# One column tiling for the matrix products of a triangle-attention stage

## The chip, the cores and the metric

The kernel runs on one core of one Trainium2 chip. The metric is the device time of one launch in microseconds (us), the median of several runs. Everything is computed in float32.

Of the engines, four matter here. TensorE (PE in the profile) multiplies matrices: a "stationary" operand is loaded into its array of 128 rows and 128 columns, and a "moving" operand streams through; results go to PSUM, an accumulation memory. VectorE (DVE) and GpSimd (POOL) do elementwise work, and ScalarE (ACT) does activations and copies.

## What is computed

Four images of 64 x 64 positions with 256 channels pass two layers. Layer 0 is a self-attention over the 4096 positions of an image (and isn't touched by the change). Layer 1 is a triangle attention followed by a small perceptron. Cut to what matters:

```python
# layer 0: x = x + attention(x) @ Wo + bo      (per image, 4096 tokens)
# layer 1, x_in = the result of layer 0, H = 8 heads of d_k = 32:
q, k, v1, v2 = (x_in @ W).reshape(B, N, N, H, d_k)   # for each of Wq, Wk, Wv1, Wv2
scores = einsum('bilhd,bljhd->biljh', q, k) / sqrt(d_k)
att = softmax(scores, axis=2)
out = einsum('biljh,bilhd,bljhd->bijhd', att, v1, v2)
h = x_in + out.reshape(B, N, N, E) @ Wo              # "hp" in the kernel
h = layer_norm(h)
mlp = relu(h @ W1 + b1) @ W2 + b2                    # "mp", then "zp"
return layer_norm(mlp + h)
```

The three-fold sum `out` is made by elementwise products of `att` and `v2` (tiles `R` on VectorE, `Rp` on GpSimd) that TensorE then sums with `v1` as its stationary operand (tile `acc`).

## The kernel before

The kernel orders its instructions by hand. While the triangle steps of image b run, the token part (hp, mp, zp: 16 tiles of 256 tokens for an image) of image b-1 runs beside them. This order repeats every two triangle steps, which the text calls a period; each period takes one tile of 256 tokens through the token part:

```python
ORDER = """
    r0/1 AO0/2 AO1/2 m1/1 RO4/2 RE5/1 SO/1 ... sp/1 ... z0/1 WO/1 ... z1/1 tO/1 ... tE ... h1/-1 ... h0/-1 ht
    ... m0 VE
""".split()      # R: product, A: accumulate, t: transposes of the weights, sp: scores,
                 # h0/h1: heads, ht: transposes of h, m0/m1: hidden, z0/z1: outputs
```

The triangle steps' work on TensorE. `accumulate` uses stationary operands of 128 rows and 32 columns, and four of them, each with its own 32 columns of the array and its own 32 partitions of PSUM, stand beside each other:

```python
def accumulate(self, step, m):
    ...
    for c in range(4):
        nc.tensor.matmul(
            acc[32 * c : 32 * c + 32, n % 2, :], w[:, n, c, 16 * h : 16 * h + 32],
            R[:, ts(c, 8), :].rearrange("p d j -> p (d j)"),
            start=n not in begun, stop=n in begun,
        )                                             # 512 moving columns

def turn_weights(self, step):                         # "att": full transposes
    for n in range(4):
        nc.tensor.transpose(att[:, n, :], e[...], ident)

def scores(self, pair, u):                            # "sp": 32 rows, 64 columns
    for n in range(8):
        for h in range(2):
            for lh in range(2):
                nc.tensor.matmul(sp[ts(h, 64), lh, n, :], k[rows, u * 8 + n, :], q[rows, u * 8 + n, :],
                                 start=True, stop=True)
```

The token part, with stationary operands of 128 columns and with transposes that add a residual to what a product has left in PSUM:

```python
def heads(self, tt, n, psum=pb, new=None):            # "hp", n = 0 and 1
    for cc in range(2):
        nc.tensor.matmul(hp[:, n, :], A[:, cc, ts(n, 2), :].rearrange("p i j -> p (i j)"), wo1_sb[:, cc, :],
                         start=(cc == 0), stop=False)
    for cc in range(2):
        nc.tensor.matmul(hp[:, n, ts(cc, P)], yc[:, cc, ts(n, P)], ident, start=False, stop=(cc == 1),
                         is_transpose=True)

def turn(self, tt):                                   # "htp"
    for cc in range(2):
        for n in range(2):
            nc.tensor.transpose(htp[:, cc, ts(n, P)], h[:, n, ts(cc, P)], ident)

def hidden(self, tt, fc, wide=False):                 # "mp", fc = 0 to 3
    for cc in range(2):
        nc.tensor.matmul(self.mp[:, fc % 2, :], w1_sb[:, cc, ts(fc, P)], self.hT[tt][:, cc, :],
                         start=(cc == 0), stop=(cc == 1))

def outputs(self, tt, n, apart=None, new=None):       # "zp", n = 0 and 1
    for fc in range(4):
        nc.tensor.matmul(zp[:, n, :], self.hid[tt][:, fc, ts(n, P)], w2_sb[:, fc, :],
                         start=(fc == 0), stop=(fc == 3 and tt not in self.hT2))
    if tt in self.hT2:
        for cc in range(2):
            nc.tensor.matmul(zp[:, n, ts(cc, P)], self.hT2[tt][:, cc, ts(n, P)], ident,
                             start=False, stop=(cc == 1), is_transpose=True)
```

Image 0 has no earlier image; beside its triangle steps (`first_layer1`) the kernel prepares layer 0 of the later images (`Ahead`): transposes of x ("tp"), values ("vp") and factors ("gf"):

```python
def values(self, s):                                  # "vp<-wh,xT"
    for n in range(4):
        for cc in range(2):
            nc.tensor.matmul(self.vp[:, ts(n, P)], self.xT[cc][:, ts(n, P)], wh_sb[:, cc, :],
                             start=(cc == 0), stop=(cc == 1))

def factors(ps, xT, t):                               # "gf", 32 stationary columns
    for w, wt in enumerate((wg_sb, wf_sb)):
        for cc in range(2):
            for n in range(4):
                nc.tensor.matmul(ps[32 * n : 32 * n + 32, w, :], wt[:, cc, :], xT[cc][:, ts(n, P)],
                                 start=(cc == 0), stop=(cc == 1))
```

The images follow one another; after the last one, `rest.alone` runs the token part of that image by itself:

```python
for b in range(NB):                                   # NB = 4
    L = layer0(b, F, safe, rest)
    ...
    if b == 0:
        first_layer1(L, ahead, F)
    else:
        next_layer1(b, L, rest, ahead, F)
    ...
rest.alone(NP * (NB - 1), NP * NB)
```

Of the kernel before, what the change touches and what calls it, by code (L numbers as in the profile page):

```python
# [16 lines left out]
P = 128  # L17
# [32 lines left out]
def attention_then_triangle_kernel(  # L50
# [6 lines left out]
    nc = tc.nc  # L57
# [13 lines left out]
    def pa(name):  # L71
        return psA.tile([P, 2, 512], F32, tag="a", name=name)

    def pb(name):
        return psB.tile([P, 512], F32, tag="b", name=name)
# [5 lines left out]
        return const.tile(shape, F32, tag=name, name=name)  # L81

    scale1 = 1.0 / math.sqrt(D)

# [212 lines left out]
    class Ahead:  # L299
# [32 lines left out]
        def values(self, s):  # L332
            self.vp = pb("vp")
            for n in range(4):
                for cc in range(2):
                    nc.tensor.matmul(
                        self.vp[:, ts(n, P)], self.xT[cc][:, ts(n, P)], wh_sb[:, cc, :],
                        start=(cc == 0), stop=(cc == 1),
                    )
# [38 lines left out]
    def layer0(b, F, safe, rest):  # L378
# [208 lines left out]
        for g in range(8 * NQB):  # L587
            qb, k = divmod(g, 8)
            if b == 0 and not safe:
                for load in later[3 * g : 3 * g + 3]:  # L590
                    load()
                if g == 6:
                    fold_bias()
                if g == 20:
                    add_b2()
            if safe and k == 0 and qb + 1 < NQB:
                mx, todo = pieces(qb + 1)
                for qc, t in todo:
                    max_piece(qc, t, mx)
                row[qb + 1] = max_row(mx)  # L600
            if g + 1 < 8 * NQB:
                scores(g + 1)
            values(g)

            if qb > 0 and not (qb == last and k >= 6):
                for part in parts[k]:
                    part(qb - 1)
            if qb == last and k == 3:
                L.fetch_v1(0)
                L.fetch_v1(1)  # L610
            if qb == last and k == 5:
                if b > 0:
                    rest.load(NP * (b - 1))
                L.fetch_qk(0, True)
# [47 lines left out]
        values1(1)  # L662
        score(2)
        hidden(0)
        score(3)
        proj(last, "q", 1, None, stage[1][:, 3, :], nc.scalar)
        L.sums(0)
        proj(last, "k", 1, None, stage[2][:, 0, :], nc.scalar)
        L.fetch_qk(1)
        L.weights(0)  # L670
        hidden(1)
        L.turn(0)
        L.stationary(0)
# [196 lines left out]
    class Tokens:  # L870
# [25 lines left out]
        def heads(self, tt, n, psum=pb, new=None):  # L896
            if n == 0 if new is None else new:
                self.hps[tt] = psum("hp").rearrange("p (n c) -> p n c", n=2)
            hp = self.hps[tt]
            A, yc = self.A[tt]  # L900
            for cc in range(2):
                nc.tensor.matmul(  # L902
                    hp[:, n, :], A[:, cc, ts(n, 2), :].rearrange("p i j -> p (i j)"), wo1_sb[:, cc, :],
                    start=(cc == 0), stop=False,
                )
            for cc in range(2):
                nc.tensor.matmul(
                    hp[:, n, ts(cc, P)], yc[:, cc, ts(n, P)], ident, start=False, stop=(cc == 1),
                    is_transpose=True,
                )  # L910


# [107 lines left out]
        def hidden(self, tt, fc, wide=False):  # L1020
            if wide and fc == 0:
                self.wide = pa("mp").rearrange("p o (f t) -> p o f t", f=2)
            if fc % 2 == 0:
                self.mp = self.wide[:, fc // 2] if wide else pb("mp").rearrange("p (f t) -> p f t", f=2)
            for cc in range(2):
                nc.tensor.matmul(  # L1026
                    self.mp[:, fc % 2, :], w1_sb[:, cc, ts(fc, P)], self.hT[tt][:, cc, :],
                    start=(cc == 0), stop=(cc == 1),
                )
            return self.mp  # L1030
# [8 lines left out]
        def outputs(self, tt, n, apart=None, new=None):  # L1039
            if n == 0 if new is None else new:  # L1040
                self.zp[tt] = pb("zp").rearrange("p (n c) -> p n c", n=2)
            zp = self.zp[tt]
            if apart is not None:
                zp = self.zp[tt + 1] = apart("zp").rearrange("p (n c) -> p n c", n=2)
            for fc in range(4):
                nc.tensor.matmul(  # L1046
                    zp[:, n, :], self.hid[tt][:, fc, ts(n, P)], w2_sb[:, fc, :],
                    start=(fc == 0), stop=(fc == 3 and tt not in self.hT2),
                )
            if tt in self.hT2:  # L1050
                for cc in range(2):
                    nc.tensor.matmul(
                        zp[:, n, ts(cc, P)], self.hT2[tt][:, cc, ts(n, P)], ident,
                        start=False, stop=(cc == 1), is_transpose=True,
                    )

        def finish(self, tt, eng=nc.gpsimd):
# [324 lines left out]
    def run(safe):  # L1382
        rest, ahead = Tokens(), Ahead()
        with tc.manual_schedule():
            F = front0(0)
            for b in range(NB):
                L = layer0(b, F, safe, rest)
                F = Front() if b + 1 < NB else None
                if F is None:

                    rest.ios.append(L.io)
                if b == 0:
                    first_layer1(L, ahead, F)
                else:
                    next_layer1(b, L, rest, ahead, F)
                if F is not None:
                    rest.ios.append(L.io)
            rest.alone(NP * (NB - 1), NP * NB)

    run(safe=False)  # L1400


# [11 lines left out]
    with tc.If(flag > 0):  # L1414
        run(safe=True)
# [33 lines left out]
```

## Time and profile before

| | before |
|---|---|
| time, median of 3 runs | 3816.12 us (3815.49 to 3818.42) |
| span of the profiled execution | 3813.2 us |
| PE busy | 3683.6 us (97%) |
| DVE busy | 2641.8 us (69%) |
| ACT busy | 1935.7 us (51%) |
| POOL busy | 1804.3 us (47%) |

The page of the profile gives each engine's busy time over the whole span, which mixes stages with different limits. Two more views split it: the busy time of each engine in a stretch of the span, and the chain of work that ended last, which follows the end of the program back to what released each step. A row such as `L1026 PE MATMUL mp<-hT,w 128*128 128x256 f32 x1024` reads: line 1026 of the kernel, TensorE, tile mp made from hT and w, stationary operand of 128 rows and 128 columns, moving operand of 128 partitions and 256 columns, 1024 records. The program has 512 such products before: the profile holds two records for a float32 product (two passes), and one for a float32 transpose. In the timeline, consecutive records of one kind are merged into a row, with the start first and the length second; as matmuls are pipelined, rows overlap, and the distance from one row's start to the next one's start is the time that the work took.

### The profile page before, as it was taken

Reading aid. Unit: us, or ns where it says so; the run is one execution under the profiler, and the core shown is the slowest. Engines: PE = TensorE matmul, PEld = TensorE weight load, DVE = VectorE, ACT = ScalarE, POOL = GpSimd, SP = SyncE. Lnnn points to the kernel's source line nnn. Section 1 sums busy time; section 2 is a strip of 40 time slices with the busy share of each in tenths; the row PEclk is TensorE's granted clock in tenths of the full one; section 3 lists DMA queues with packets and bytes.
Section 4 is the critical chain, followed back from the end, with each engine's and each line's share of the span. In section 5 each row is a group of like instructions: output and inputs, shape, how many; then the busy total and the mean of one; then the engine's idle time right before and its main releaser. Section 6 shows DMA issues by size and latency. Waiting matters only on the chain.

```text
span 3813.2 us, 60145 instructions
## 1 busy us (share of the span) xinstructions
PE 3683.6 (97%) x23498; PEld 1796.9 (47%) x23498; DVE 2641.8 (69%) x2050; ACT 1935.7 (51%) x4257; POOL 1804.3 (47%) x930
## 2 busy tenths in 40 slices
PE   9999988898999999999999999999999999999997
PEld 5444443443444455554344445555344445555476
DVE  4444488897544459999544548999754455999976
ACT  3333355554333357676333346766533335677654
POOL 4000088896000049999200008999600004999954
PEclk9999999999999999999999999999999999999999
DMA  4111355544111164323111143342211116431221
GB/s 117 54 50 49 97 140 139 150 114 152 36 47 53 50 151 92 86 57 94 62 47 50 50 125 89 81 95 70 92 42 47 50 60 142 95 89 48 69 61 51
DMA packets 439749, 309.43 MB, mean 81 GB/s; under 512 B 299360, under 2 KB 404576, under 8 KB 432160
## 3 DMA queue, kind: packets, MB, share of 16 engines
q1 hardware_dynamic: 419952, 291.12, 29.0%
q10 hardware_dynamic: 16240, 8.59, 0.9%
q0 software_dynamic: 3264, 5.78, 0.6%
q8 instruction: 188, 3.08, 0.4%
q14 instruction: 105, 0.86, 0.1%
HBM read 165.88 MB, written 139.46 MB: 80 GB/s over the span
## 4 chain that ended last, share of the span: by engine, by line
PE 81%; POOL 7%; issue 3%; DMA 3%; DVE 3%; ACT 3%; SPq 0%; ACTq 0%; POOLq 0%; DVEq 0%
PE o L453 24%; PE acc L843 17%; PE proj L510 8%; PE s L431 7%; POOL Rp L833 6%; PE mp L1026 5%; PE zp L1046 5%; PE sp L731 3%; PE v1p L535 3%; PE hp L902 2%; PE y L495 2%; DVE R L833 1%; PE att L785 1%; ACT S L741 1%; PE den L470 1%
## 5 line engine op out<-in xcount | busy, mean ns | idle before, releaser
L833 POOL TENSOR_TENSOR Rp<-attP,v 128x2048 f32<-128x2048 f32 x328 | 1490.1, 4574 | 462.4 <-DMA qk<-k 327.2
L833 DVE TENSOR_TENSOR R<-att,v 128x2048 f32<-128x2048 f32 x696 | 1548.9, 2274 | 113.7 <-PE acc L843 76.6
L460 DVE TENSOR_TENSOR esum<-esum,e 128x2048 f32<-128x2048 f32 x224 | 512.8, 2289 | 583.0 <-ACT e L442 579.8
L843 PE MATMUL acc<-R,wsel 128*32 128x512 f32 x5568 | 711.0, 605 | 44.2 <-DVE R L833 32.1
L442 ACT ACTIVATE e<-s 128x1024 f32<-128x1024 f32 x512 | 496.8, 1022 | 403.0 <-PE s L431 385.4
L954 POOL TENSOR_SCALAR nt<-mv 128x4 f32<-128x4 f32 (+1 forms) x51 | 9.9, 193 | 1283.3 <-DVE mv L919 1279.5
L453 PE MATMUL o<-e,vlo 128*128 128x512 f32 x1024 | 473.7, 605 | 0.0
L453 PE MATMUL o<-e,vhi 128*128 128x512 f32 x1024 | 472.6, 605 | 0.0
L853 ACT COPY ao<-acc 128x1024 f32<-128x1024 f32 x256 | 255.4, 1021 | 229.1 <-PE acc L843 202.5
L843 PE MATMUL acc<-Rp,wsel 128*32 128x512 f32 x2624 | 345.5, 600 | 21.3 <-POOL Rp L833 21.0
L843 PEld LDWEIGHTS acc<-R,wsel 128*32 128x32 f32 x5568 | 153.7, 110 | 381.5 <-issue 263.1
L453 PEld LDWEIGHTS o<-e,vlo 128*128 128x128 f32 x1024 | 184.0, 189 | 280.8 <-issue 280.8
L453 PEld LDWEIGHTS o<-e,vhi 128*128 128x128 f32 x1024 | 184.3, 189 | 279.7 <-issue 279.7
L431 PE MATMUL s<-gT,fT 32*128 32x512 f32 x2048 | 302.3, 640 | 4.3 <-ACT e L442 4.0
L768 ACT ACTIVATE es<-S,rd 128x64 f32<-128x64 f32 x1024 | 257.7, 336 | 10.2 <-DVE rd L760 7.0
L472 DVE RECIPROCAL rec<-den 128x512 f32<-128x512 f32 x32 | 107.4, 3357 | 215.6 <-PE den L470 215.6
L1046 PE MATMUL zp<-w,hid 128*128 128x256 f32 x1024 | 247.5, 387 | 7.2 <-ACT hid L1035 7.2
L1026 PE MATMUL mp<-hT,w 128*128 128x256 f32 x1024 | 249.5, 389 | 0.7 <-ACT hT L998 0.7
L1026 PEld LDWEIGHTS mp<-hT,w 128*128 128x128 f32 x1024 | 186.5, 190 | 101.4 <-ACT hid L1035 36.9
L1046 PEld LDWEIGHTS zp<-w,hid 128*128 128x128 f32 x1024 | 186.4, 191 | 71.9 <-issue 31.9
L522 ACT COPY st<-proj 128x512 f32<-128x512 f32 x104 | 61.0, 586 | 293.1 <-issue 165.9
L843 PEld LDWEIGHTS acc<-Rp,wsel 128*32 128x32 f32 x2624 | 81.1, 111 | 211.7 <-issue 140.6
(166 smaller groups left out, 3826.7 us busy)
## 6 DMA issues: line engine op xcount, KB each, us to landing
v<-v2d SPq DMA_DIRECT2D x24, 1024.0 KB, 12.5
v1c<-v1d SPq DMA_DIRECT2D x128, 128.0 KB, 2.8
aT<-ao SPq DMA_DIRECT2D x1024, 16.0 KB, 1.9
A<-aT SPq DMA_DIRECT2D x256, 64.0 KB, 2.1
out_dram<-z SPq DMA_DIRECT2D x63, 256.0 KB, 2.5
y<-yT SPq DMA_DIRECT2D x56, 256.0 KB, 2.1
q<-st SPq DMA_DIRECT2D x56, 256.0 KB, 2.5
v1d<-st SPq DMA_DIRECT2D x56, 256.0 KB, 2.2
```

What stands on the lines that cost most here:

```text
L431: nc.tensor.matmul(s_ps[r // 2][:, r % 2, :], fT[rows, tt, ts(n, P)], gT[rows, ts(qb, QB)], start=True, stop=not safe,)
L442: nc.scalar.activation(e[g][:, 2 * j : 2 * j + 2, :], s_ps[j], AF.Exp)
L453: nc.tensor.matmul(o_ps[qb], F.v[tt][:, r * 4 + n, :], es[:, r, :], start=(k == 0 and r == 0), stop=(k == 7 and r == 3),)
L460: nc.vector.tensor_tensor(esum[qb], esum[qb], es, ALU.add)
L510: nc.tensor.matmul(ps, w[:, cc, rows], y(qb, cc), start=(cc == 0), stop=(cc == 1))
L535: nc.tensor.matmul(ps[:, ts(n, C)], y(qb, cc)[:, ts(m * 2 + n, P)], wv1_sb[:, cc, :], start=(cc == 0), stop=(cc == 1),)
L768: nc.scalar.mul(e[:, i, :], rows[:, i, :], rec[:, i : i + 1])
L833: eng.tensor_tensor(R, src.unsqueeze(1).to_broadcast([P, D, N]), v2[:, h], ALU.mult)
L843: nc.tensor.matmul(acc[32 * c : 32 * c + 32, n % 2, :], w[:, n, c, 16 * h : 16 * h + 32], R[:, ts(c, 8), :].rearrange("p d j -> p (d j)"), ...
L853: nc.scalar.copy(self.ao[step][:, ts(np, 2)].rearrange("p k d j -> p k (d j)"), self.acc[step][np])
L1026: nc.tensor.matmul(self.mp[:, fc % 2, :], w1_sb[:, cc, ts(fc, P)], self.hT[tt][:, cc, :], start=(cc == 0), stop=(cc == 1),)
L1046: nc.tensor.matmul(zp[:, n, :], self.hid[tt][:, fc, ts(n, P)], w2_sb[:, fc, :], start=(fc == 0), stop=(fc == 3 and tt not in self.hT2),)
```

## The change

The products of the token part and of `values` are divided, wherever they run inside the triangle steps, into four products of 32 stationary columns each, so that TensorE's array has there the same division into four times 32 columns as for `accumulate`. The residuals, which were transposes, become ordinary products with the identity (divided in the same way). It is for having fewer changes of the array's division between neighbouring pieces of work. Outside the triangle steps (`tiling[0] = 1`) everything is as it was. The diff, with cuts marked:

```diff
+    tiling = [1]
+
+    def mm(out, lhsT, rhs, start, stop, residual=False):
+        m = P // tiling[0]
+        how = dict(is_transpose=True) if residual and tiling[0] == 1 else {}
+        for c in range(tiling[0]):
+            nc.tensor.matmul(out[ts(c, m)], lhsT[:, ts(c, m)], rhs, start=start, stop=stop, **how)
 ...                                            # Ahead.values
-                    nc.tensor.matmul(
+                    mm(
                         self.vp[:, ts(n, P)], self.xT[cc][:, ts(n, P)], wh_sb[:, cc, :],
 ...                                            # heads
-                nc.tensor.matmul(
+                mm(
                     hp[:, n, :], A[:, cc, ts(n, 2), :].rearrange("p i j -> p (i j)"), wo1_sb[:, cc, :],
                     start=(cc == 0), stop=False,
                 )
             for cc in range(2):
-                nc.tensor.matmul(
+                mm(
                     hp[:, n, ts(cc, P)], yc[:, cc, ts(n, P)], ident, start=False, stop=(cc == 1),
-                    is_transpose=True,
+                    residual=True,
                 )
 ...                                            # hidden
-                nc.tensor.matmul(
+                mm(
                     self.mp[:, fc % 2, :], w1_sb[:, cc, ts(fc, P)], self.hT[tt][:, cc, :],
 ...                                            # outputs: the products, and the residuals
-                nc.tensor.matmul(
+                mm(
                     zp[:, n, :], self.hid[tt][:, fc, ts(n, P)], w2_sb[:, fc, :],
 ...
-                    nc.tensor.matmul(
+                    mm(
                         zp[:, n, ts(cc, P)], self.hT2[tt][:, cc, ts(n, P)], ident,
-                        start=False, stop=(cc == 1), is_transpose=True,
+                        start=False, stop=(cc == 1), residual=True,
                     )
 ...                                            # the loop over images
+                tiling[0] = 4
                 if b == 0:
                     first_layer1(L, ahead, F)
                 else:
                     next_layer1(b, L, rest, ahead, F)
+                tiling[0] = 1
```

## The prediction

> **What bounds the kernel now.** I read the page first, then the chain of work that ended last, then the busy times by stretch, then the timeline of TensorE.
>
> ```profile
> PE 3683.6 (97%) x23498; PEld 1796.9 (47%) x23498; DVE 2641.8 (69%) x2050; ACT 1935.7 (51%) x4257; POOL 1804.3 (47%) x930
> ```
>
> TensorE is busy for 97% of the span, but the change touches only the triangle steps, so the question is what bounds those. The chain of waits shows it: in image 1 pieces of `acc` begin at 1429.59, 1457.35, 1485.11 ... 1707.21, that is every 27.76 us, and between them the chain stays on PE. From about 1729 us on it passes to POOL (59% of the chain from 1730 to 1785). Images 2 and 3 repeat this (PE from 2300 to 2629 and from 3201 to 3533). In image 0 (about 480 to 900) it hops between DMA, POOL, DVE, ACT and PE. The busy times of three stretches, one period of the first kind, one of the second, and two triangle steps of image 0; the columns after the length are PE, PEld, DVE, ACT, POOL:
>
> ```profile
> 1540.63:1568.39 27.76, 27.76 (x257) 14.96 (x260) 26.86 (x20) 19.65 (x55) 26.64 (x15) 1.00 0.20 49
> 1756.00:1783.20 27.20, 26.30 (x189) 13.09 (x189) 26.99 (x20) 17.60 (x53) 26.55 (x15) 1.00 0.32 88
> 600.00:626.20 26.20, 18.88 (x224) 8.56 (x224) 25.43 (x17) 13.60 (x36) 26.05 (x6) 0.99 0.85 189
> ```
>
> In the first PE is busy in all of 27.76 us, DVE is 0.90 us short of it, POOL 1.12. In the second PE has 0.9 us to spare (there are no more scores to make), and DVE and POOL are full. In image 0 PE idles for 7 of 26 us. So a change of PE's work counts in full in the first kind, about 12 periods in each of images 1 to 3 (1729 less 1400, over 27.76, is 11.9), 36 in all; in the others little of it.
>
> Now the first kind of period itself. Row by row the timeline of PE gives the work and, from one start to the next, its cost:
>
> ```profile
> 1545.85 0.66 PE L785 MATMUL att<-ident,es 128*128 128x128 f32 x4
> 1546.34 1.03 PE L902 MATMUL hp<-wo,A 128*128 128x256 f32 x4
> 1547.21 0.38 PE L907 MATMUL hp<-ident,yc 128*128 128x128 f32 x2
> 1547.43 1.03 PE L902 MATMUL hp<-wo,A 128*128 128x256 f32 x4
> 1548.29 0.38 PE L907 MATMUL hp<-ident,yc 128*128 128x128 f32 x2
> 1548.51 0.60 PE L993 MATMUL htp<-ident,h 128*128 128x128 f32 x4
> 1549.04 1.92 PE L843 MATMUL acc<-R,wsel 128*32 128x512 f32 x16
> 1550.78 1.04 PE L843 MATMUL acc<-Rp,wsel 128*32 128x512 f32 x8
> 1551.76 1.99 PE L1026 MATMUL mp<-hT,w 128*128 128x256 f32 x8
> 1553.68 1.92 PE L843 MATMUL acc<-R,wsel 128*32 128x512 f32 x16
> 1555.53 1.99 PE L1026 MATMUL mp<-hT,w 128*128 128x256 f32 x8
> 1557.46 1.98 PE L731 MATMUL sp<-qk 32*64 32x64 f32 x64
> 1559.37 1.07 PE L843 MATMUL acc<-R,wsel 128*32 128x512 f32 x8
> ...
> 1563.80 1.99 PE L1046 MATMUL zp<-w,hid 128*128 128x256 f32 x8
> 1565.63 0.38 PE L1052 MATMUL zp<-ident,hT 128*128 128x128 f32 x2
> 1565.85 1.89 PE L1046 MATMUL zp<-w,hid 128*128 128x256 f32 x8
> 1567.58 0.38 PE L1052 MATMUL zp<-ident,hT 128*128 128x128 f32 x2
> ```
>
> The reader is to see three things. A full record of 256 columns costs 0.216 us (1565.85 to 1567.58, 1.73 over 8). A transpose of 128 columns costs 0.109 (0.22 over 2). And a piece after a change of the array's division costs more: the first eight zp records take 1.83, the second eight 1.73. The starts of the single records give the rest. Four `acc` records begin within 20 ns, and the next four 429 ns later, so four narrow records of 512 columns pass in 429 ns. By the same starts a change costs:
> - from 32 columns to full products 217 ns (the last four narrow ones are followed after 542 in place of 429, the first full one after 320 in place of 216);
> - from 32 columns to transposes 170 (543 and 165, against 429 and 109);
> - from 128 columns to 32 columns 118 (93 and 25);
> - from mp to the scores 111, from the scores to `acc` 145.
> Between transposes and full products there is none.
>
> The sum proves the parts: 32 quadruples of `acc` x 0.429 = 13.73; 40 full records x 0.216 = 8.64; 20 transposes x 0.109 = 2.18; 16 quadruples of scores x 0.111 = 1.78; nine changes (acc to att, htp to acc, acc to mp, mp to acc, acc to mp, mp to sp, sp to acc, acc to zp, att to acc) = 0.170 + 0.118 + 0.217 + 0.118 + 0.217 + 0.111 + 0.145 + 0.217 + 0.118 = 1.43. Together 27.76, which is the period.
>
> **What the Trainium skill says.** "TensorEngine Tiling (Array Packing)", Key Properties: a change of the tiling mode drains TensorE, a change of the tile alone doesn't. The trace agrees, with 111 to 217 ns each. The same page, Gotcha 2: column tiling excludes the transpose mode for float32 inputs; that is why the residuals must become ordinary products. "TensorE: Matmul & The Clock Gate", Terms, has the transpose mode four times faster for float32. Here it is twice: `vp` products of 128 columns go at 111 ns a record with two records a product, a transpose is one record of 109. The measurement decides. The same page, Part 3, "The mechanism": tiles start about 4 ns apart and run together. The trace has 7 ns for the four tiles.
>
> **The change, part by part.** The changed program has TensorE's work in the same order, each full product replaced in its place by four narrow ones.
>
> (a) Full products: 20 a period, 40 records of 216 ns, become 40 quadruples. No full quadruple of 256 columns stands in the trace, but its neighbours do: 429 ns at 512 columns, and 109 at 128 in the factors of image 0, which are shown here (16 records, four quadruples, from 640.64 to 641.08):
>
> ```profile
> 640.64 0.62 PE L227 MATMUL gf<-xT,wf 128*32 128x128 f32 x16
> 641.08 1.04 PE L843 MATMUL acc<-R,wsel 128*32 128x512 f32 x8
> ```
>
> Halfway by columns lies 109 + 128 x (429 - 109)/384 = 216 ns, the full record's own time. The weights' loads are hidden in both. So (a) is 0.
>
> (b) Residuals: 8 transposes of one record, 8 x 0.109 = 0.87, become 8 products of two passes, 16 quadruples x 0.109 = 1.74. That adds 0.87.
>
> (c) Changes of division. Gone: acc to mp twice (0.434), mp to acc (0.118), acc to zp (0.217), 0.77 in sum. New: `att` and `htp` stay full transposes, and hp now stands between them with 32 columns: att to hp (0.118), hp to htp (0.170); and zp to the next att (0.170): 0.46. From mp to sp I take 0.13 in place of 0.11. Nine changes become eight, and 1.43 becomes 1.14: 0.29 less.
>
> Sum: 0.87 - 0.29 = +0.58 us a period, 28.34 in place of 27.76, as PE is the bound and stays it. 36 x 0.58 = +21 us.
>
> (d) The periods bound by POOL (about four in each of images 1 to 3): PE's +0.6 fits in its 0.9 of slack: 0 to +2 us in all.
>
> (e) Image 0: 24 runs of `values`, each now 16 quadruples x 0.109 = 1.74 in place of 1.98 from start to start and 0.14 of change before and after it: 0.38 less, 9 us at most. But POOL (26.05 of 26.20) and DVE (25.43) are full there, so I take -2.
>
> 3816 + 21 - 2 = 3835 us.
>
> **The rivals.** *The drains win*: the residuals' second pass costs nothing, or a drain costs more than its starts show. Then -0.29 a period or somewhat more, about 3804. For it: it is what the change is meant for. Against it: one change out of nine goes, and the factors show two passes at full price. A floor stands below it: DVE needs 26.86 of the 27.76, so no more than 0.9 x 36 = 32 us can be won before DVE is the bound, 3784, which is 0.8%. Faster by 2% isn't to be had. *The quadruples are slow*: in `acc` and in the factors each of the four has its own moving data, here the four share one, and a quadruple of 256 columns doesn't occur. If one took 240 in place of 216, 40 x 0.024 = +0.96 a period more, 3870; to be slower by 2% (76 us, 2.1 a period) it would have to take 254. For it: more loads and records for PE to take in (four times as many in these rows); against it: the factors take theirs at 109 a quadruple, twice that rate. *PE's growth is hidden*: then nothing changes, 3816. Against it: PE has no idle time in the first kind of period.
>
> **Range and chances.** The main sum gives 3835. Half the residuals' cost or another 0.1 for each of some drains moves it by 15 each way; the rivals stretch it upward more than downward. I take 3815 to 3853 for eight in ten. Faster by over 2% is ruled out by DVE but for what I don't see: 0.01. Slower by over 2% needs the slow quadruples: 0.05. Within 2%: 0.94.
>
> **What would show each step right or wrong.** Period of 28.3 us, PE busy in all of it, DVE still near 26.9. mp as eight quadruples in 1.73 us with no 217 ns before it; zp's residuals 0.44 us for two, not 0.22; 0.12 from att to hp and 0.17 from hp to htp. If the quadruples of 256 columns are not 0.216 apart, step (a) is wrong; if the residuals take one pass, (b); if the period is under 27.76, the drains weigh more than I read; if image 0 is shorter by over 5 us, (e).

## The result and the profile after

The changed kernel takes 3832.8 us (median, 3830.94 to 3837.54) against 3817.2 for the kernel before on the same chip: a ratio of 1.0043, with a 95% interval from 1.0026 to 1.0060, or 10 to 23 us more. It is slower by a small amount that can be told from none.

The page's busy times after the change:

```profile
PE 3696.4 (96%) x32794; PEld 1744.9 (46%) x32794; DVE 2643.3 (69%) x2050; ACT 1930.3 (50%) x4257; POOL 1810.5 (47%) x930
```

40% more records than before (32794 for 23498) in nearly the same busy time: four narrow records pass together in the time of one. The busy times of the two kinds of period (columns PE, PEld, DVE, ACT, POOL after the length; then the granted clock, 1.00 as before, the DMA share and GB/s):

```profile
1571.24:1599.57 28.33, 28.33 (x432) 13.77 (x436) 26.95 (x20) 19.49 (x55) 26.76 (x15) 1.00 0.47 106
1756.00:1783.20 27.20, 26.81 (x375) 12.13 (x371) 26.99 (x20) 17.81 (x53) 26.55 (x15) 1.00 0.40 91
```

In the first, PE is still busy in all of the period, which is now 28.33 us long, and DVE and POOL have the same work as before with more room. In the second, PE's work grew from 26.30 to 26.81 us and still fits. The timeline of TensorE in that first period; as before, the distance from one start to the next is what the work took:

```profile
1576.46 0.65 PE L796 MATMUL att<-ident,es 128*128 128x128 f32 x4
1577.04 1.07 PE L94 MATMUL hp<-wo,A 128*32 128x256 f32 x16
1577.93 0.62 PE L94 MATMUL hp<-ident,yc 128*32 128x128 f32 x16
1578.37 1.05 PE L94 MATMUL hp<-wo,A 128*32 128x256 f32 x16
1579.23 0.62 PE L94 MATMUL hp<-ident,yc 128*32 128x128 f32 x16
1579.78 0.66 PE L1004 MATMUL htp<-ident,h 128*128 128x128 f32 x4
1580.37 1.92 PE L854 MATMUL acc<-R,wsel 128*32 128x512 f32 x16
...
1582.97 1.91 PE L94 MATMUL mp<-hT,w 128*32 128x256 f32 x32
1584.69 1.90 PE L854 MATMUL acc<-R,wsel 128*32 128x512 f32 x16
1586.41 1.91 PE L94 MATMUL mp<-hT,w 128*32 128x256 f32 x32
1588.25 1.98 PE L742 MATMUL sp<-qk 32*64 32x64 f32 x64
...
1594.48 1.91 PE L94 MATMUL zp<-w,hid 128*32 128x256 f32 x32
1596.20 0.62 PE L94 MATMUL zp<-ident,hT 128*32 128x128 f32 x16
1596.64 1.91 PE L94 MATMUL zp<-w,hid 128*32 128x256 f32 x32
1598.37 0.62 PE L94 MATMUL zp<-ident,hT 128*32 128x128 f32 x16
1598.92 0.66 PE L796 MATMUL att<-ident,es 128*128 128x128 f32 x4
```

`mp` takes 1.72 us for eight groups of four narrow records ("quadruples"), about 0.216 each, and the `acc` records between its two parts take 1.72 where they took 1.85: no change of division is left there. The first products of `zp` take 1.72 where they took 1.83. The residuals of `hp` and of `zp` (16 records, four quadruples) take 0.44 where they took 0.22. And the pieces around the transposes have grown: from the first `att` to `hp` 0.58 where it was 0.49, and from the second residuals to `htp`, and from those of `zp` to `att`, 0.55, which is 0.44 for the records and 0.11 for the change behind them (0.22 before, with no change). The distance between two rows shows only a part of a change; the other part is in the row behind it: `htp` takes 0.59 to the next `acc` where it took 0.53, which brings the 0.11 to the 0.17 of the prediction.

By stages, from the records of the two profiled executions (their spans are 3813.2 and 3832.8 us):

| stage | before | after | difference |
|---|---|---|---|
| image 0: up to its last `acc` | 926.95 | 923.59 | -3.4 |
| images 1 to 3: first `acc` to start of the last record of scores, sum | 937.97 | 958.25 | +20.3 |
| images 1 to 3: from there to last `acc`, sum | 402.09 | 405.10 | +3.0 |
| all else (layer 0 of images 1 to 3, the end) | 1546.2 | 1545.9 | -0.3 |

### The profile page after: what moved, and what is told of

Same layout as the page of the kernel before. It is cut to its first block, busy times and chain, and to the rows that moved or that the text cites. A ratio compares the mean times of both kernels' runs of the same rounds, so it can differ in the third digit from the quotient of the medians.

```text
span 3832.8 us, 78704 instructions
## 1 busy us (share of the span) xinstructions
PE 3696.4 (96%) x32794; PEld 1744.9 (46%) x32794; DVE 2643.3 (69%) x2050; ACT 1930.3 (50%) x4257; POOL 1810.5 (47%) x930
## 4 chain that ended last, share of the span: by engine, by line
PE 82%; POOL 5%; DVE 5%; DMA 3%; ACT 2%; issue 2%; SPq 1%; ACTq 0%; POOLq 0%; DVEq 0%
PE o L464 24%; PE acc L854 17%; PE proj L521 8%; PE s L442 7%; PE zp L94 5%; PE mp L94 4%; POOL Rp L844 4%; PE hp L94 3%; PE sp L742 3%; DVE R L844 3%; PE v1p L546 3%; PE y L506 1%; PE att L796 1%; ACT S L752 1%; PE htp L1004 1%
## 5 line engine op out<-in xcount | busy, mean ns | idle before, releaser
L94 PE MATMUL zp<-w,hid 128*32 128x256 f32 (+1 forms) x3328 | 246.0, 380 | 7.2 <-ACT hid L1046 7.2
L94 PE MATMUL mp<-hT,w 128*32 128x256 f32 (+1 forms) x3232 | 241.8, 379 | 1.0 <-ACT hT L1009 1.0
L94 PEld LDWEIGHTS mp<-hT,w 128*32 128x32 f32 (+1 forms) x3232 | 150.5, 117 | 113.2 <-issue 29.8
L94 PEld LDWEIGHTS zp<-w,hid 128*32 128x32 f32 (+1 forms) x3328 | 149.1, 116 | 93.4 <-issue 24.9
```

Of the source, the lines that this page charges most:

```text
L94: nc.tensor.matmul(out[ts(c, m)], lhsT[:, ts(c, m)], rhs, start=start, stop=stop, **how)
```

## The experiments

All kernels are the changed one with another `mm`. It is told which part calls it, and divides only some parts:

```diff
+    DIVIDED = ("mp",)                  # this line is what differs
-    def mm(out, lhsT, rhs, start, stop, residual=False):
-        m = P // tiling[0]
-        how = dict(is_transpose=True) if residual and tiling[0] == 1 else {}
-        for c in range(tiling[0]):
+    def mm(part, out, lhsT, rhs, start, stop, residual=False):
+        t = tiling[0] if part in DIVIDED else 1
+        m = P // t
+        how = dict(is_transpose=True) if residual and t == 1 else {}
+        for c in range(t):
             nc.tensor.matmul(out[ts(c, m)], lhsT[:, ts(c, m)], rhs, start=start, stop=stop, **how)
```

"Period" below is the distance between the first records of two neighbouring groups of scores in images 1 to 3 (nine such distances an image, after the first two, in which the pipeline fills); the median is given where nothing else is said. By this measure the kernel before has 27.76 and the changed one 28.34. The main theory is the prediction's: TensorE bounds these periods, and its time is records plus changes of division. Its rival is that the number of records costs.

### mp_only: the part without residuals

The edit is the listing above. 

> Only the mp products are divided into four of 32 columns; hp, zp and values and all residuals stay as before. Main theory (the time is the sum of the changes of division and of the residuals' second pass): acc to mp twice and mp to acc go, 0.217 + 0.217 + 0.118 = 0.55 us a period, mp to the scores grows by 0.02, no residual is touched: period 27.23 in place of 27.76 us, 36 x -0.53 = -19, about 3798 us. Rival (what costs is the number of TensorE's records, 0.58 us for 172 more records a period, 3.4 ns each): 48 more records, +0.16 a period, about 3823.

Measured: 3796.5 us against 3811.2 for the kernel before on the same chip, ratio 0.9962 (0.9949 to 0.9976), so 15 us less (9 to 19), where 19 were expected. Faster than both kernels. The first four periods of each image are 27.23, as expected, the last ones 27.3. The timeline:

```profile
1470.90 1.04 PE L857 MATMUL acc<-Rp,wsel 128*32 128x512 f32 x8
1471.76 1.91 PE L97 MATMUL mp<-hT,w 128*32 128x256 f32 x32
1473.48 1.90 PE L857 MATMUL acc<-R,wsel 128*32 128x512 f32 x16
1475.20 1.91 PE L97 MATMUL mp<-hT,w 128*32 128x256 f32 x32
1477.04 1.21 PE L745 MATMUL sp<-qk 32*64 32x64 f32 x36
```

`acc` 0.86 for two quadruples, `mp` 1.72, `acc` 1.72, `mp` 1.84 with the change to the scores at its end. The rival by number of records falls: 48 more records a period, and less time. The 27.3 of the later periods is a wait at `hp`: its first records start at 1684.54, right behind the last of ScalarE's reading of `zp` (1683.46 plus 1.02), which itself had waited 0.59 us for a GpSimd result. The row of `hp` is 1.12 long there, and 1.03 in a period of 27.23:

```profile
1683.46 1.02 ACT L984 ACTIVATE z<-zp,rn 128x256 f32<-128x256 f32 x2 [0.59 <-POOL rn L979]
1684.54 1.12 PE L97 MATMUL hp<-wo,A 128*128 128x256 f32 x4
```

That is the next limit. It takes back 0.07 of the 0.53 us.

### hp_only and zp_only: the parts with residuals

`DIVIDED = ("hp",)` and `DIVIDED = ("zp",)`. 

> Only hp's products are divided, with their residuals as products with the identity. Main theory: four residuals get a second pass, +0.44 us a period; att to hp and hp to htp are new changes of division, 0.118 + 0.170 = 0.29, none goes: +0.72, period 28.48, about 3843 us. Rival (number of records): 52 more, +0.18, 27.94, about 3823.

> Only zp's products are divided, with their residuals as products with the identity. Main theory: +0.44 for the residuals' second pass, acc to zp goes (-0.217), zp to att comes (+0.170): +0.39 us a period, 28.15, about 3831. Rival (number of records): 76 more, +0.26, 28.02, about 3826.

Measured: hp alone 1.0084 (1.0070 to 1.0098), period 28.48; zp alone 1.0043 (1.0029 to 1.0056), period 28.15. Both median periods are the expected ones to the last digit, and the rival's 27.94 and 28.02 are not. In hp alone, the last residual is seen with a doubled time and a new change behind it, 0.55 us from 1555.48 to 1556.03 (0.22 before the change):

```profile
1554.62 1.05 PE L97 MATMUL hp<-wo,A 128*32 128x256 f32 x16
1555.48 0.62 PE L97 MATMUL hp<-ident,yc 128*32 128x128 f32 x16
1556.03 0.66 PE L1007 MATMUL htp<-ident,h 128*128 128x128 f32 x4
```

The three parts' differences of period, -0.53, +0.72 and +0.39, sum to +0.58, the whole change's. hp alone costs 32 us in all by its ratio, where 36 x 0.72 = 26 was expected. Its profiled span is 30.6 us longer (3843.8 for 3813.2): 19.4 in the 27 periods, 3.6 in the starts of the three images, 2.9 behind their last scores, and 4.7 in image 0 and all else, which the division of hp doesn't touch. So a part is scatter; the rest isn't settled.

### ident_full: the residuals' second pass by itself

```diff
     def mm(part, out, lhsT, rhs, start, stop, residual=False):
-        m = P // tiling[0]
         how = dict(is_transpose=True) if residual and tiling[0] == 1 else {}
-        for c in range(tiling[0]):
-            nc.tensor.matmul(out[ts(c, m)], ...)
+        nc.tensor.matmul(out, lhsT, rhs, start=start, stop=stop, **how)
```

> Nothing is divided; only the residuals in the triangle steps become ordinary products with the identity, with 128 stationary columns. Main theory: 8 transposes of 0.109 become 16 records of 0.111, +0.90 us a period and no change of division more or less: 28.66, about 3849 us. Rival (number of records): 8 more records, +0.03, 27.79, about 3818. Second rival (the second pass is cheap when undivided): below +0.3 a period, under 3828.

Measured: 1.0081 (1.0068 to 1.0095), +31 us; period 28.67. Two residuals are four records here and take 0.45 us:

```profile
1550.91 0.61 PE L92 MATMUL hp<-ident,yc 128*128 128x128 f32 x4
1551.36 1.03 PE L92 MATMUL hp<-wo,A 128*128 128x256 f32 x4
```

So the second pass costs what the prediction put on it, and more than the whole change does. Both rivals named in the expectation fall.

### turned_residuals: the same division, residuals left as transposes

```diff
+        t = 1 if residual else tiling[0]
+        how = dict(is_transpose=True) if residual else {}
```

> As the changed kernel, but the residuals stay undivided transposes between the divided products. Main theory: the residuals' second pass goes (-0.87 us a period against the changed kernel), and five changes of division come back around them in hp and zp (32 columns to transposes three times and back twice more, less the one at htp and the one at att that they replace, net +0.58): 28.05 us a period, 0.29 above the kernel before and 0.29 below the changed one, about 10 us above the kernel before. Rival (number of records): 56 fewer than in the changed kernel, 28.15, but the same rival has missed before; a rival in which a drain costs less between pieces of 32 columns and transposes would show under 27.9.

Measured: 1.0020 (1.0010 to 1.0029), +8 us; period 28.04. The price moved from the second pass into changes of division:

```profile
1548.74 0.44 PE L95 MATMUL hp<-ident,yc 128*128 128x128 f32 x2
1549.11 1.07 PE L95 MATMUL hp<-wo,A 128*32 128x256 f32 x16
1550.11 0.44 PE L95 MATMUL hp<-ident,yc 128*128 128x128 f32 x2
```

The two residuals with the change behind them take 0.37 (1548.74 to 1549.11), the products between them 1.00 where 0.86 would do. It is 0.30 us a period less than the changed kernel and 0.28 more than the kernel before.

### all_narrow: in images 1 to 3 one division for everything but the scores

`DIVIDED = ("hp", "zp", "mp", "vp", "att", "htp")`, and `nc.tensor.transpose` in `turn_weights` and `turn` replaced by `mm("att", ..., residual=True)` and `mm("htp", ..., residual=True)`. 

> As the changed kernel, and the transposes att and htp become divided products with the identity too, so that only the scores have another division. Main theory: 12 transposes of 0.109 become 24 quadruples, +1.31 us a period, and all changes but those around the scores (0.13 + 0.145) go, 0.86: 28.79 a period, about +37 us over the kernel before. If one tiling for everything were worth more than its transposes, the period would be below the changed kernel's 28.34.

Measured: 1.0126 (1.0111 to 1.0141), +48 us (42 to 54) where 37 were expected, the slowest of all. 20 of its 27 periods are 28.78, as expected. Seven are longer, 29.1 to 30.0, by 7 us in sum, which is most of the difference; one of them is shown at the end. So carrying the idea through costs still more: 12 more transposes a period had to be given up, at 1.31 us, for 0.86 us of changes.

### mp_64: narrow, but another division

`t = 2 if part == "mp" and tiling[0] == 4 else 1`. 

> Only mp is divided, into two products of 64 columns: narrower than before, but not the division of acc. Main theory: the changes between acc and mp stay; only the second part of the change into mp (0.104, which I put down to the load of 128 columns) may shrink: 27.6 to 27.76 us a period, at most 6 us below the kernel before. Rival (narrow stationary operands are quicker by themselves, whatever their neighbours' division): 27.3, as with mp in four.

Measured: 1.0002 (0.9994 to 1.0010), no difference; period 27.67.

```profile
1555.71 1.95 PE L95 MATMUL mp<-hT,w 128*64 128x256 f32 x16
1557.59 1.92 PE L855 MATMUL acc<-R,wsel 128*32 128x512 f32 x16
1559.45 1.95 PE L95 MATMUL mp<-hT,w 128*64 128x256 f32 x16
```

From `mp` to `acc` 1.88 us (1.92 before the change, 1.72 when divided into four), and the `acc` between takes 1.86 (1.85 before the change). So the gain of mp_only is not in narrowness: with 64 columns, which isn't the neighbours' division, it isn't there. The rival's 27.3 falls. The small difference, 0.09 a period, came as the smaller load was expected to give it, but that cause is only argued.

### vp_only, mp_vp and mp_vp_zp0: image 0, and the best version

`DIVIDED = ("vp",)` and `DIVIDED = ("mp", "vp")`; in the third also the zp products with `n == 0`, with all residuals left as undivided transposes. 

> Only values (image 0) is divided into four. Main theory: TensorE saves 0.38 us at each of 24 places, about 0.3 of it shows in the 26.75 us from one scores to the next of image 0 (26.4 in all kernels so far that divide values), 2 to 4 us in all; images 1 to 3 stay at 27.76. About 3 below the kernel before, near the limit of what can be told. Rival (POOL and DVE, full there, take all of it): 26.75 and no change.

> mp and values divided into four, hp and zp as before. Main theory: the sum of the two alone: periods of 27.23 to 27.3 us, image 0 at 26.4: 15 to 18 below the kernel before.

> mp, values and the first half of zp's products divided into four, all residuals left as undivided transposes. Main theory: mp alone gives 27.23 and was held at 27.3 in later periods by hp's first records; the first half of zp takes the change from before the zp products (0.217) to before its residuals (0.170), -0.05 on TensorE, which that wait takes back; image 0 gains 3 us from values. About 3 us below mp alone, 18 below the kernel before. Rival: the wait at hp comes later by as much as TensorE comes earlier, then only image 0 shows anything.

Measured: vp alone 0.9996 (0.9988 to 1.0004); mp and vp 0.9964 (0.9953 to 0.9975); with half of zp 0.9972 (0.9961 to 0.9983). In image 0 dividing `values` shortens the usual distance between two groups of scores from 26.75 to 26.43 us, but three of its twelve distances, about 35 us each, grew by 0.2 to 1.5. In the last two of these TensorE's transposes of x wait for the transfer of `xin`, 5.1 and 4.4 us in the kernel before and 6.5 and 6.7 in vp_only, and GpSimd and VectorE wait behind TensorE: TensorE works less, and waits longer. No gain of the time could be told. With half of zp the first two periods are 27.18, then 27.3, held by the same wait at `hp`: what TensorE wins there is taken back. Mp and vp together were expected 15 to 18 us below the kernel before and are 14 below (10 to 18); with half of zp 18 was expected and 11 (6 to 15) came, which is a miss. The gain of image 0 that this expectation counted on, and that could not be told, is 3 of the 7; the rest isn't explained. The three versions with mp divided can't be told from each other; all beat the kernel before by 0.3 to 0.4%, and mp alone is the simplest.

## Why the prediction was right

The time was foretold as 3835, 19 us more than before, and is 3832.8, 16 us more (10 to 23). Point by point:

- **The bound** was right. PE is busy in all of the first kind of period before and after, and the experiments moved these periods by what TensorE's sum says, or, once it fell to 27.2, were held by the wait at `hp`. The floor that the prediction put at DVE's 26.9 was too low; the wait comes first, at 27.3.
- **The 36 periods** are not shown. 27 distances between scores are settled ones, and these grew by 16.1 us (27 x 0.58 is 15.7). The other 4.2 of the stage's 20.3 lie in the start of each image, from the first `acc` to the third group of scores. That stretch, summed over the three images, lies between 177 and 187 us in the twelve profiles and doesn't follow TensorE's work: it is 6.1 shorter than before in zp_only, whose periods grew by 0.39, and the same in ident_full, whose periods grew by 0.91. So the 0.58 of a period is confirmed, and that 36 x 0.58 met the stage's 20.3 so closely is in part luck.
- **(a) Full products: 0.** `mp` passes eight quadruples in 1.72 us; that they share their moving data costs nothing. The estimate of 216 ns between 109 and 429 was the measured number.
- **(b) Residuals: +0.87.** ident_full has the undivided form by itself, +0.91 where 0.90 was expected, and the divided form is seen in the timeline, 0.44 for 0.22, four times a period.
- **(c) Changes of division: -0.29.** The whole period came out at 28.34, which needs it; hp_only, zp_only and mp_only confirm its three shares, and turned_residuals and all_narrow the price of each change in other orders (28.04 and 28.78, where 28.05 and 28.79 were expected).
- **(d)** was put at 0 to +2 and was +3.0 in the profiles. That TensorE's growth is the reason isn't shown: mp_only, in which TensorE's work shrank, has the same +3.0 behind the last scores. **(e)** was put at -2 and was -3.4 in the profiles; alone, (e) is -1.5 us with an interval from -5 to +2, so its size isn't settled. The first scores of image 0, with nothing changed ahead of them, start at 470.1 us before, at 469.3 in the changed kernel and at 474.8 in vp_only, which is more than the size in question. The two errors are of opposite sign.
- **Of the rivals,** *the drains win* was wrong for the whole and right for one part: where products stand between two pieces of the same division and have no residual (mp), the gain was there, 0.53 us a period. *The quadruples are slow* and *PE's growth is hidden* have nothing for them in the periods of any run.

The table of periods, the sum of the parts against the measurement:

| kernel | sum of the parts, us | measured, us | ratio of times |
|---|---|---|---|
| mp_only | 27.23 | 27.23, later 27.3 | 0.9962 |
| mp_64 | 27.6 to 27.76 | 27.67 | 1.0002 |
| turned_residuals | 28.05 | 28.04 | 1.0020 |
| zp_only | 28.15 | 28.15 | 1.0043 |
| the change | 28.34 | 28.34 | 1.0043 |
| hp_only | 28.48 | 28.48 | 1.0084 |
| ident_full | 28.66 | 28.67 | 1.0081 |
| all_narrow | 28.79 | 28.78, seven of 27 longer | 1.0126 |

## What to carry to other kernels

Before giving neighbouring products one division of the array, count the changes in the real order of the instructions, those that the new neighbours bring as well as those that go: here nine became eight. In these traces a round trip between 32 columns and transposes costs 0.29 us, and a float32 transpose turned into a product 0.11 us more for each 128 columns, so a trip is worth at most two of them. Divide only the pieces that lie between neighbours of that division and need no transpose.

## What the runs showed that was not expected

In all_narrow seven periods were longer, and one such place shows how four column tiles can fall out of step. Of two groups of four `acc` records only three each start before TensorE stops, with 0.25 us idle for which the profile names no wait. Then the two missing ones come one after the other, at 1494.51 and 1494.94, while the other three go on with the next product (`Rp`), so one of the four columns is two records behind:

```profile
1492.37 1.89 PE L858 MATMUL acc<-R,wsel 128*32 128x512 f32 x14
1494.51 0.59 PE L858 MATMUL acc<-R,wsel 128*32 128x512 f32 x1 [0.25 <-issue]
1494.52 0.63 PE L858 MATMUL acc<-Rp,wsel 128*32 128x512 f32 x3
1494.94 0.59 PE L858 MATMUL acc<-R,wsel 128*32 128x512 f32 x1
```

One and three alternate from there to the scores, 15 us later, behind which the four start together again. The period took 1.26 us more: 0.41 at the stop, and the other 0.85 is about two records of 0.43, the lag of the one column. Why TensorE stopped isn't shown. Four stops of more than 0.6 us in this kernel's periods each came 1.2 to 1.7 us after the landing of a 16 KB instruction transfer that was about 12 us behind the one before it, but other intervals as long (12.6 and 13.0 us in image 3) were followed by no such stop, and no run tried it.
